# Four-layer scan network: where VectorE's side work stands beside each scan, which buffer takes the product with C, and how finely the side work is cut

## The chip, the cores and the metric

The kernel runs on one core of a Trainium2 chip. The metric is device time in microseconds (us) of one launch. PE is TensorE, DVE is VectorE, ACT is ScalarE, POOL is GpSimd, SP is SyncE, which issues all the DMAs here. Each engine executes its own instructions strictly in the order in which the program lists them; an instruction that waits holds up everything behind it on its engine.

## The reference

Four images of 64 x 64 pixels with 96 channels go through four layers. Each layer is a token mixer and a feed-forward, both with a residual:

```
x = x + conv_ref(ln_c(x))          # layer 0: gated linear recurrence; layers 1-3: selective scan
t = t + ffn_ref(ln_t(t))           # quantised 96 -> 384 -> 96 with relu
```

The mixer of layers 1 to 3 projects 96 channels to 192 plus a gate z, applies a 3x3 depthwise convolution and silu, and then runs four scans over the 4096 pixels: two pixel orders (by rows, by columns), each in both directions. Each of 192 channels has 16 states:

```
def step(h, inp):
    u_l, dl, b_l, c_l = inp
    dA = jnp.exp(dl[..., None] * A)
    h = dA * h + (dl * u_l)[..., None] * b_l[:, :, None, :]
    y = jnp.einsum('bkdn,bkn->bkd', h, c_l)
    return (h, y)
```

The four results are added, normalised, gated with silu(z) and projected back to 96 channels.

## The kernel before, in words

**Tiles of the scan.** A scan tile covers 128 rows (two halves of 64 channels, one in each pixel order), 1024 pixels and one of the 16 states. One image and layer has 2 directions x 4 segments x 3 chunks x 16 states = 384 tiles. A stage is one image in one layer; 3 layers x 4 images make 12 stages, and `scans` (lines 855 to 1036) runs all 12 x 384 = 4608 tiles in one loop over k. `CHUNKS` says which channels and pixel order the halves of the three chunks have.

**One tile on the engines.** SP broadcasts C's row of this state from DRAM into the buffer `c` (`c_rows`, two DMAs). ACT makes `da` = exp(delta x A) (`decays`). PE spreads B's row over the partitions into PSUM `bc` (`b_rows`, two matmuls). DVE multiplies `bc` by `du` in place, which I call the product, and runs the scan into `h` (both in `scan`). ACT copies the scan's last column to `carry`, for the next segment (`carry`). POOL multiplies h by c (`times_c`), here in place into h. PE adds the result into the accumulator `acc` (`accumulate`, eight matmuls), and after 16 states ACT copies `acc` out and SP stores it (`store`).

**Order in the loop.** In pass k the program emits, in this order: carry(k-1), C's rows and decays of k+2, B's rows of k+1, the product and the scan of k, times_c(k-1), sometimes a store, then the side work, then accumulate(k-2). All engines go in order, so on DVE the side work of pass k stands behind scan k and ahead of product k+1; on PE it stands between B's rows of k+1 and accumulate(k-2).

**Side work.** Three things are generators that hand out a few instructions and then `yield`: `prepare_chunk` (delta and du of the next chunk), `next_segment` (projections to B and C of the next segment), and the job. A pass takes one piece of each of the first two, and `work()` takes pieces of the job. The job of a stage, `between(im, layer)`, is everything that lies between two scans for the next image: joining the four results (`join_orders`, chain `joins`), norm, gate and output projection (`mixer_out`), `feed_forward`, then `take_in` and `convolve`. Up to three chains of it run side by side. `Job.step` adds `rate` to a credit in each pass (1.4, or 1.9 for the last feed-forwards; the credit is capped at 2.0), and every whole credit pumps each chain once. So a `yield` more in a chain means one round more, and `rate` is rounds per tile. A piece that needs a PSUM bank yields `True` and is only taken when one is free.

**The end of a job.** At item 22 of 24 of a stage, state 4 (tile 356), lines 999 to 1003 take all of the job that is left at once, with no scans between. The last image's feed-forward, which follows the last scan, has nothing beside it. The feed-forwards of images 0 and 1 in layer 3 are jobs that open once stage 10's own job is done, that of image 2 is in stage 11 behind them, that of image 3 runs after all scans (line 1282). What is left of jobs after the last tile runs in lines 1034 to 1036.

**Buffers.** `sb(n, tag, ...)` takes the next of n buffers in turn, and waits until the readers of its last use are done. h has four, freed by accumulate; c has four, freed by times_c. POOL's times_c writes over h, so it also has to wait until ACT has read h for the carry.

**Layer 0.** `gated` (lines 1039 to 1262) runs 32 strips x 12 tiles in a similar loop. From tile 96 on it has the job of image 0 beside it, at the default rate of 1.4.

## Time and profile before

| | us |
|---|---|
| median of 3 runs | 20146.27 (20117.64 to 20146.91) |
| the profiled execution's own time | 20152.58 |
| its span, first to last instruction | 20150.8 |
| DVE busy in it | 17808.5 (88%) |
| POOL busy in it | 15531.3 (77%) |
| PE busy in it (matmul records) | 16417.6 (81%) |
| ACT busy in it | 12295.0 (61%) |
| first wide scan starts, last one ends | 1890.3, 19679.4 |

The span has three parts: layer 0 with the first preparation up to 1890 us; the 4608 scan tiles, 17,789 us; and 471 us after the last scan, in which DVE is nearly idle. Rows of groups read: line, engine, operation, output <- inputs with shapes, count | busy us, mean ns of one | idle us of that engine just before them, and what ended it. All instructions are issued by a helper in line 80, so groups are told apart by the names of tiles.

### The profile page before, as it was taken

The page shows a single profiled execution, that of the slowest core. Times are in us where ns is not written, and L with a number is a line of the kernel's source. Part 1 is how long each engine was busy: PE and PEld are TensorE (multiplying, and loading weights), DVE is VectorE, ACT ScalarE, POOL GpSimd, SP SyncE. Part 2 cuts the span into 40 slices and gives each one's busy share as a digit, 9 for nine tenths or more (in the row PEclk, how much of TensorE's full clock was granted, in tenths as well). Part 3 has the DMA queues.
Part 4 walks back from the last instruction along what each step waited for, and adds up shares of the span by engine and source line. Part 5 has one row for each costly group of instructions (what it writes and reads, how often), then busy time and mean ns, then how long its engine had stood idle before and what let it go on. Part 6 is the DMA issues. An engine that isn't in the chain of part 4 may idle for free. (4 is left out here: it accounts for less than half of the span.)

```text
span 20150.8 us, 220842 instructions
## 1 busy us (share of the span) xinstructions
PE 16417.6 (81%) x70656; PEld 4838.3 (24%) x70656; DVE 17808.5 (88%) x13848; ACT 12295.0 (61%) x19373; POOL 15531.3 (77%) x10470
## 2 busy tenths in 40 slices
PE   8998788787888787788788888788788888887776
PEld 3332121121122222222222222222222222222223
DVE  6665999999999998999999999989999999999881
ACT  4444665665665665665665666666666666666553
POOL 3434888888888887888888888878888888878882
PEclk9898796786887797897887887887887887888775
DMA  0002666666666666666666676666676666676661
GB/s 20 16 18 69 165 181 174 166 186 167 168 184 171 164 179 175 166 182 180 167 187 171 167 189 167 169 180 169 170 187 171 168 187 168 170 188 161 172 169 44
DMA packets 1234532, 3148.68 MB, mean 156 GB/s; under 512 B 428049, under 2 KB 428177, under 8 KB 1227217
## 3 DMA queue, kind: packets, MB, share of 16 engines
q1 hardware_dynamic: 1233360, 3134.55, 58.6%
q8 instruction: 554, 9.08, 0.2%
q14 instruction: 618, 5.05, 0.1%
HBM read 2819.18 MB, written 314.57 MB: 156 GB/s over the span
## 5 line engine op out<-in xcount | busy, mean ns | idle before, releaser
L80 POOL TENSOR_TENSOR h<-h,c 128x1024 f32<-128x1024 f32 x4608 | 10834.6, 2358 | 2827.5 <-ACT carry L80 1727.5
L80 DVE TENSOR_TENSOR_SCAN h<-da,carry,bc 128x1024 f32<-128x1024 f32 x4608 | 10814.5, 2347 | 608.7 <-POOL carry L80 10.3
L80 PE MATMUL acc<-h,stacked 64*64 64x512 f32 x36864 | 6179.1, 747 | 498.7 <-POOL h L80 493.8
L80 ACT ACTIVATE da<-delta,decay 128x1024 f32<-128x1024 f32 x4608 | 5280.9, 1147 | 1648.9 <-DVE h L80 1601.8
L80 DVE TENSOR_TENSOR bc<-du,bc 128x1024 f32<-128x1024 f32 x4608 | 5574.5, 1210 | 611.2 <-PE bc L80 586.0
L80 PE MATMUL bc<-bs,sel 96*128 96x512 bf16 x9216 | 3346.9, 451 | 2071.8 <-DVE h L80 2054.6
L80 ACT COPY carry<-h 128x1 f32<-128x1 f32 x3456 | 649.0, 188 | 3533.7 <-DVE h L80 3529.1
L80 PEld LDWEIGHTS <-sel 96*128 96x128 bf16 x9216 | 551.3, 101 | 6988.6 <-DVE h L80 5085.7
L80 PEld LDWEIGHTS acc<-h,stacked 64*64 64x64 f32 x36864 | 1132.5, 153 | 3286.5 <-issue 1699.7
L80 ACT ACT_TABLE_LOAD x1133 | 1453.6, 1283 | 41.6 <-DVE mv L80 22.5
L80 POOL TENSOR_TENSOR c<-h,c 128x512 f32<-128x512 f32 x384 | 485.7, 1265 | 970.5 <-ACT c L80 614.8
L80 PE MATMUL conv<-pad,tap_lo 128*128 128x512 f32 x1728 | 917.5, 630 | 0.0
L80 PE MATMUL dt_proj<-rows,w 12*128 12x512 f32 x1152 | 828.0, 805 | 0.0
L80 ACT ACTIVATE du<-e,ones 128x1024 f32<-128x1024 f32 x576 | 660.8, 1147 | 228.8 <-POOL delta L80 223.2
L80 PE MATMUL x_proj_b<-u,xp 128*108 128x512 f32 x1152 | 671.9, 699 | 94.3 <-DMA xp<-in_ssm 59.0
L80 ACT ACTIVATE c<-c,l_bias 128x512 f32<-128x512 f32 x384 | 263.5, 686 | 753.0 <-PE c L80 737.9
L80 POOL TENSOR_TENSOR delta<-delta,du 128x1024 f32<-128x1024 f32 x288 | 679.5, 2359 | 12.1 <-ACT du L80 12.1
L80 POOL TENSOR_TENSOR e<-e,du 128x1024 f32<-128x1024 f32 x288 | 679.4, 2359 | 2.4 <-ACT du L80 2.4
L80 POOL TENSOR_TENSOR du<-delta,u 128x1024 f32<-128x1024 f32 x288 | 679.4, 2359 | 0.7
L80 POOL TENSOR_TENSOR delta<-delta,e 128x1024 f32<-128x1024 f32 x288 | 678.5, 2356 | 0.1
L80 PE MATMUL x_proj_c<-u,xp 128*48 128x512 f32 x1152 | 624.3, 655 | 64.3 <-ACT rows L80 64.3
L80 PE MATMUL conv<-pad,tap_hi 128*128 128x512 f32 (+1 forms) x1152 | 638.5, 650 | 8.2 <-ACT u L80 8.2
(155 smaller groups left out, 16118.3 us busy)
## 6 DMA issues: line engine op xcount, KB each, us to landing
c<-cs SPq DMA_DIRECT2D x9216, 256.0 KB, 4.1
u<-u SPq DMA_DIRECT2D x288, 512.0 KB, 7.6
y<-y SPq DMA_DIRECT2D x1152, 128.0 KB, 2.4
y<-y SPq DMA_DIRECT2D x144, 512.0 KB, 5.6
xr<-x SPq DMA_DIRECT2D x224, 192.0 KB, 4.8
u<-u SPq DMA_DIRECT2D x288, 128.0 KB, 4.4
pad<-y SPq DMA_DIRECT2D x288, 128.0 KB, 4.6
z<-zl SPq DMA_DIRECT2D x96, 256.0 KB, 2.0
```

The lines of the kernel that those rows point to most:

```text
L80: ins = f(*a, **k).ins
```

## The change

The edits, in groups:

- DVE's order: the side work of pass k is emitted between the product and the scan of k (`beside()`), no longer behind the scan. The log calls of the norms stand behind carry and decays; the start values of a chunk's carry are set at state 8 of the chunk before (`start`).
- Buffers: times_c writes into c, not h. So h is freed by times_c and the carry, and has three buffers; c is freed by accumulate, and has six. accumulate lags the scan by three tiles, not two; the loop is one pass longer.
- Finer side work: the norm's statistics are handed out two groups at a time, with the aggregates in a piece of their own; empty yields are added in `join_orders`, `mixer_out`, `feed_forward`, `first`. The rates go from 1.4 to 1.65, from 1.9 to 2.6, and in layer 0 from 1.4 to 2.6; the cap of the credit from 2.0 to 3.0.
- Smaller things: the four POOL additions of the bias in `feed_forward` become one with a broadcast operand; its result x2 shares the single buffer `xh`; the second chunk's halves are swapped, so that C needs 32 projected rows, not 48, and B's selection matrix 128 columns, not 192; `stacked` is a part of `twice`. In layer 0 h has three buffers and c six.

The diff, cut to its core (the addresses of the swapped halves and the host's packing of the weights are left out):

```diff
-CHUNKS = (((0, 0), (64, 1)), ((0, 1), (64, 0)), ((128, 0), (128, 1)))
+CHUNKS = (((0, 0), (64, 1)), ((64, 0), (0, 1)), ((128, 0), (128, 1)))
...
 NB3 = 96
-NC3 = 48
-XPW = NB3 + 2 * R + NC3
+NC2 = 2 * NS
+XPW = NB3 + 2 * R + NC2
...
-        n: ctx.enter_context(tc.tile_pool(name=f"sb{n}", bufs=n)) for n in (1, 2, 3, 4, 5, 13)
+        n: ctx.enter_context(tc.tile_pool(name=f"sb{n}", bufs=n)) for n in (1, 2, 3, 4, 5, 6, 13)
...
-    sel = const("sel", [NB3, NS, 192], BF16)
+    sel = const("sel", [NB3, NS, 128], BF16)
     for n in range(NS):
-        for k in range(3):
-            at = NS * (k % 2) + n
+        for k in range(2):
+            at = NS * k + n
             dve.tensor_copy(
                 sel[:, n, 64 * k : 64 * k + 64], mod32[:, at : at + 1].to_broadcast([NB3, 64])
...
-    def moments(src, width):
-
-        st = sb(5, "st", [128, G, 6])
-        mv = sb(5, "mv", [128, G, 2])
-        for g in range(G):
-            dve.bn_stats(st[:, g, :], src[:, g, 0:width])
-        for g in range(G):
-            dve.bn_aggr(mv[:, g, :], st[:, g, :])
-        return mv
...
@@ -226,7 +214,14 @@
 
         def measure(self, src, width, e):
 
-            mv = moments(src, width)
+            st = sb(5, "st", [128, G, 6])
+            mv = sb(5, "mv", [128, G, 2])
+            for g in range(G):
+                dve.bn_stats(st[:, g, :], src[:, g, 0:width])
+                if g % 2:
+                    yield
+            for g in range(G):
+                dve.bn_aggr(mv[:, g, :], st[:, g, :])
             yield
             act.activation(self.v, mv[:, :, 1], AF.Identity, bias=small[e])
...
             release()
             yield pair == 0
+        yield
...
         yield
         normalise(yt, yt, DI, norm.r, norm.nm)
+        yield
         yield True
...
                 pool.tensor_tensor(v[0:m], v[0:m], z[0:m], ALU.mult)
-                yield m == 64
+                yield
+        yield True
         ps = bank("out_proj")
         for q in range(G):
...
             pe.matmul(o, g[1][0:64, t], w[0:64, W_OUT + C : W_OUT + 2 * C], start=False, stop=True)
             yield
+        yield
         x1 = sb(2, "x1", [128, G, C])
         dve.tensor_tensor(x1, xr, ps[:, 0 : G * C].rearrange("p (g c) -> p g c", g=G), ALU.add)
         release()
...
         sp.dma_start(out=yc, in_=im.y[2, 0:64, t])
         sp.dma_start(out=yr[0:64], in_=im.y[0, 0:64, t])
-        sp.dma_start(out=yr[64:128], in_=im.y[1, 64:128, t])
+        sp.dma_start(out=yr[64:128], in_=im.y[1, 0:64, t])
...
         yield
         xh = sb(1, "xh", [128, G, C])
         normalise(xh, x1, C, norm.r, norm.nm)
+        yield
         yield True
         ps = bank("ff_xt")
         transpose_strip(ps, xh, 0, C)
+        yield
+        yield
         yield
         xq = sb(1, "xq", [C, MM], F8)
         dve.tensor_copy(xq, ps[0:C], saturate=False)
...
         pool.tensor_copy(hq[:, 2, :], late, saturate=False)
+        yield
         yield True
         ps = bank("ff_y")
...
         yield
-        for g in range(G):
-            pool.tensor_tensor(y[:, g, :], y[:, g, :], b[:, 3 : 3 + C], ALU.add)
-        yield
-        x2 = sb(1, "x2", [128, G, C])
+        pool.tensor_tensor(y, y, b[:, None, 3 : 3 + C].to_broadcast([128, G, C]), ALU.add)
+        yield
+        x2 = sb(1, "xh", [128, G, C])
         pool.tensor_tensor(x2, x1, y, ALU.add)
+        yield
         yield
         sp.dma_start(out=tokens(dst, s), in_=x2)
         if layer < 3:
+            yield
             norm = hold["norm", s] = Norm()
             yield from norm.measure(x2, C, 1e-6)
...
                     )
                 load_y(im, 0, hold)
+            yield
             yield
...
         def step(self):
-            self.credit = min(self.credit + self.rate, 2.0)
+            self.credit = min(self.credit + self.rate, 3.0)
...
@@ -752,7 +757,7 @@
             sp.dma_start(out=sg.us[c], in_=item.im.u[c, :, t])
         weights[item.layer].load_xp()
         sg.bs = sb(2, "bs", [NB3, T], BF16)
-        sg.cs = dram.tile([NC3, T], F32, tag="cs", name="cs")
+        sg.cs = dram.tile([NC2, T], F32, tag="cs", name="cs")
...
+        def start(i):
+            if i.first:
+                carries[i.chunk] = sb(2, f"carry{i.chunk}", [128, NS])
+                pool.memset(carries[i.chunk], 0.0)
+            i.carry = carries[i.chunk]
...
-            c = live[k, "c"] = sb(4, "c", [128, T])
+            c = live[k, "c"] = sb(6, "c", [128, T])
             for half in range(2):
-                row = NS * (CHUNKS[i.chunk][0][1] + half) + n
+                row = NS * half + n
...
-        def scan(k):
+        def scan(k, beside):
             i, n = tiles[k]
             da, b = live.pop((k, "da")), live.pop((k, "b"))
-            if n == 0 and i.first:
-                carries[i.chunk] = sb(2, f"carry{i.chunk}", [128, NS])
-                pool.memset(carries[i.chunk], 0.0)
-            i.carry = carries[i.chunk]
             dve.tensor_tensor(b, i.du, b, ALU.mult)
-            h = live[k, "h"] = sb(4, "h", [128, T])
+            beside()
+            h = live[k, "h"] = sb(3, "h", [128, T])
...
-            h, c = live[k, "h"], live.pop((k, "c"))
-            pool.tensor_tensor(h, h, c, ALU.mult)
+            c = live[k, "c"]
+            pool.tensor_tensor(c, live.pop((k, "h")), c, ALU.mult)
...
-            h = live.pop((k, "h"))
+            h = live.pop((k, "c"))
...
-        for k in range(last + 4):
+        for k in range(last + 5):
...
-                if n == 11:
-                    logarithms()
+                if n == 8 and nxt is not None:
+                    start(nxt)
                 if n == 8 and nxt is not None and nxt.d == 1:
                     nxt.yf = sb(2, "y", [128, T])
                     sp.dma_start(out=nxt.yf, in_=nxt.im.y[nxt.chunk, :, nxt.seg * T : (nxt.seg + 1) * T])
-            if 0 <= k - 1 <= last:
-                carry(k - 1)
-            if k + 2 <= last:
-                c_rows(k + 2)
-                decays(k + 2)
-            if k + 1 <= last:
-                b_rows(k + 1)
-            if k <= last:
-                scan(k)
-            if 0 <= k - 1 <= last:
-                times_c(k - 1)
-            if k >= 3 and (k - 3) % NS == NS - 1:
-                store(items[(k - 3) // NS])
-            if k <= last:
+            def beside():
                 pump(chain)
                 pump(segment)
                 if n == 13:
@@ -1028,8 +1023,24 @@
                     if item.chunk == 2:
                         drain(segment, work)
                 work()
-            if 0 <= k - 2 <= last:
-                accumulate(k - 2)
+
+            if 0 <= k - 1 <= last:
+                carry(k - 1)
+            if k + 2 <= last:
+                c_rows(k + 2)
+                decays(k + 2)
+            if n == 11:
+                logarithms()
+            if k + 1 <= last:
+                b_rows(k + 1)
+            if 0 <= k - 1 <= last:
+                times_c(k - 1)
+            if k >= 4 and (k - 4) % NS == NS - 1:
+                store(items[(k - 4) // NS])
+            if k <= last:
+                scan(k, beside)
+            if 0 <= k - 3 <= last:
+                accumulate(k - 3)
...
-            y = sb(4, "h", [C, MM])
+            y = sb(6, "c", [C, MM])
...
-            h = t["h"] = sb(4, "h", [128, T])[:, 0:MM]
+            h = t["h"] = sb(3, "h", [128, T])[:, 0:MM]
...
-            c = sb(4, "c", [128, T])[:, 0:MM]
+            c = sb(6, "c", [128, T])[:, 0:MM]
...
-        gated(images, Job(between(images[0], 0), patience=1), pl0)
+        gated(images, Job(between(images[0], 0), 2.6, patience=1), pl0)
...
-            jobs[-1].append(Job(between(im, layer - 1), 1.4))
+            jobs[-1].append(Job(between(im, layer - 1), 1.65))
 
         for im in {10: images[:2], 11: images[2:3]}.get(at, ()):
-            jobs[-1].append(Job(between(im, 3, im.dst), 1.9))
+            jobs[-1].append(Job(between(im, 3, im.dst), 2.6))
```

## Prediction

> **What bounds the kernel now.** I read the page first: shares of the engines, then the costliest groups and their idle time.
>
> ```profile
> PE 16417.6 (81%) x70656; PEld 4838.3 (24%) x70656; DVE 17808.5 (88%) x13848; ACT 12295.0 (61%) x19373; POOL 15531.3 (77%) x10470
> ...
> L80 POOL TENSOR_TENSOR h<-h,c 128x1024 f32<-128x1024 f32 x4608 | 10834.6, 2358 | 2827.5 <-ACT carry L80 1727.5
> L80 DVE TENSOR_TENSOR_SCAN h<-da,carry,bc 128x1024 f32<-128x1024 f32 x4608 | 10814.5, 2347 | 608.7 <-POOL carry L80 10.3
> ...
> L80 DVE TENSOR_TENSOR bc<-du,bc 128x1024 f32<-128x1024 f32 x4608 | 5574.5, 1210 | 611.2 <-PE bc L80 586.0
> ```
>
> DVE is the bound while scans run. Its idle time there has two sources of like size: 608.7 us before scans, of which almost none has a releaser (608.7 / 4608 = 0.13 us each), and 611 us before products, nearly all for B's rows from PE. The chain of waits (DVE, 1890 to 19679 us) shows how little else there is:
>
> ```profile
> DVE bc L80 <- PE bc L80: 586.0, 352, 18.0
> DVE xq L80 <- PE ff_xt L80: 24.0, 27, 1.8
> DVE bc L80 <- POOL du L80: 23.3, 1, 23.3
> ```
>
> All DVE waits over 0.15 us sum to 678 us, by stage 46, 30, 28, 74, 48, 49, 47, 77, 48, 51, 71, 109. The same tile of each stage has the same wait. Two of them on the timeline, first DVE and PE in tile 62 of stage 5:
>
> ```profile
> 9435.18 1.21 DVE L80 TENSOR_TENSOR bc<-du,bc 128x1024 f32<-128x1024 f32 x1
> 9436.52 2.35 DVE L80 TENSOR_TENSOR_SCAN h<-da,carry,bc 128x1024 f32<-128x1024 f32 x1
> 9444.34 1.23 DVE L80 TENSOR_TENSOR bc<-du,bc 128x1024 f32<-128x1024 f32 x1 [5.47 <-PE bc L80]
> ```
>
> ```profile
> 9433.31 0.60 PE L80 MATMUL bc<-bs,sel 96*128 96x512 bf16 x2
> 9438.41 0.74 PE L80 MATMUL out_proj<-w,u 128*128 128x96 f32 x2 [4.50 <-POOL u L80]
> ...
> 9443.59 0.71 PE L80 MATMUL bc<-bs,sel 96*128 96x512 bf16 x2
> ```
>
> PE stands still in the job (the output projection waits 4.50 us for POOL's gate product), and the next B rows stand behind it. Then PE and POOL in tile 300:
>
> ```profile
> 10350.95 1.00 PE L80 MATMUL bc<-bs,sel 96*128 96x512 bf16 x2
> 10355.93 1.99 PE L80 MATMUL acc<-h,stacked 64*64 64x512 f32 x8 [3.98 <-POOL h L80]
> ```
>
> ```profile
> 10348.93 2.36 POOL L80 TENSOR_TENSOR e<-e,du 128x1024 f32<-128x1024 f32 x1
> 10351.23 1.07 POOL L80 COPY cols_a<-u 128x512 f32<-128x512 f32 x1
> 10352.14 1.29 POOL L80 COPY part_c<-u 64x256 f32<-64x256 f32 x2
> 10353.52 4.66 POOL L80 TENSOR_TENSOR h<-h,c 128x1024 f32<-128x1024 f32 x2
> ```
>
> POOL lags by a row of side work, accumulate(k-2) waits 3.98 us, B's rows again stand behind (2.2 us on DVE). Undisturbed tiles start 3.60 us apart (median); 4608 x 3.60 = 16,589 of the 17,789 us, the other 1,200 are 678 of waits and 522 of side work on DVE. After the last scan there is a stretch with next to no DVE work:
>
> ```profile
> 19680.00:20151.00 471.00, 278.73 (x1348) 170.13 (x1340) 47.64 (x225) 174.68 (x380) 120.97 (x282) 0.51 0.16 39
> ```
>
> **The change part by part**
>
> *The tail.* By the rounds, image 2's last feed-forward has 336 before, some 118 of them run by the last tile (62 tiles x 1.9), and 218 follow alone. In the timeline of SP its last store is at 19858.8 us, and image 3's loads start at 19859.3 and end in the last store at 20147.7. So 179 us of the tail is a job left over. With rate 2.6 the three jobs (337, 347, 359 rounds) end in tiles 89, 228 and 372 of stage 11, before the last scan. Image 3 then waits for the last tile: POOL 2.4, accumulate 1.1 to 2, the copy of acc about 1.0, the store 2.4 us to landing, together 8; x2 in the buffer of xh makes the next strip wait for its store (2.2 us to landing), at most 8 x 2 = 16, of which I take 12, less 8 x 0.5 for the one POOL addition: 8 + 12 - 4 = 16 in all, and 16 - 179 = -163.
>
> *Job work moved into the scans.* The 218 rounds' DVE work, about 20 us (47.6 us for both jobs of the tail), +20.
>
> *Side work between product and scan.* The 0.13 us before a scan is the wait for its own product: 9435.18 + 1.21 = 9436.39, and the scan starts at 9436.52. Following the emission, 578 tiles had DVE side work before; 884 have it after, since statistics are cut finer. In these the piece fills the gap. After a non-scan the next independent instruction follows within about 0.03 us (norm aggregates to product: median 0), so 0.10 us each: -88. The Trainium skill (VectorE: DVE Perf Modes, Terms, DRAIN) speaks against it: every DVE instruction is followed by a flush, and the next can't issue until the pipe is empty. Then a piece in between would fill nothing, and the sum were 0. But a product follows an independent scan with no gap at all (9425.71 + 2.35 is 9428.06, and the next starts at 9427.97): only the dependent pair pays. I take the row, and keep 0 for the range.
>
> *What that place costs.* There the piece must have its inputs 2.48 us (0.13 + 2.35) earlier in its tile, and the scan is queued behind it, then ACT's carry and decays, then POOL. I took from the timeline each such piece's producer and compared its end with the end of the product: late in 76 of 106 xq (159 us in sum), 43 of 84 statistics of yt (47), 32 of 83 sums with out_proj (36), 12 of 190 `rows` (20). That is 262 us if nothing else moved. But the yields put two more rounds ahead of xq (1.2 tiles, 4.4 us, at 1.65) and one ahead of the next two (0.6 tile, 2.2 us); only `rows` has none. I count 20 to 40 of it.
>
> *PE's stalls.* The yields stand exactly where PE waited: ahead of the projection (5.5 us a stage in tile 62), of ff_y (3.7), of ff_xt (tiles 56, 118, 154: 6.2; the xq waits of 40, 55, 153: 3). accumulate(k-3) has a further 3.6 us, over the 4.0 of tile 300 but for a rest (2.2 us and some smaller ones, 2 to 4). The carry's start value leaves the queue of scan 224 (1.6). So of 48 us about 23 go; 25 stay: PE's bursts of joins and 16 accumulates at a chunk's start, convolutions, the loads at a job's start. The 12 leftover rounds taken at once in stages 3 and 7 (18.0 us each) end, as the jobs now finish in tile 346. Stages 0 to 10: 568 to about 260, the new waits included. Stage 11 keeps 95 of 109, since it gets the work of 866 old rounds, not 648. Together -323. From the same place two bounds: no stall ends, 0, and nearly all do, -580.
>
> *Three buffers of h.* Scan k now waits for times_c(k-3). In the trace of before times_c ended later than that scan's start in 20 of 4608 tiles, by 18.6 us together; POOL loses the 1727.5 us wait for the carry, so I take 0, up to +19. *Six of c:* C's rows of k+2 wait on SP for accumulate(k-4), no longer for times_c(k-2) (8547 us of SP's waits); SP's job loads are queued behind. They have 3 tiles, 11 us, to land in 4.1: 0. Where PE is late they come late too, but then DVE waits for B first.
>
> *POOL.* The product's form is the same (writing c costs as h: in layer 0 c<-h,c 512 wide is 1265 ns). Four additions of 367 ns become one like x<-x,ff_y, 910 ns: 0.56 us x 128 = 72 us, hidden under DVE, but for the tail counted above. The Trainium skill (SBUF — State Buffer, SBUF: two separate sides) has an exclusive lock between GpSimd and a DVE instruction with two SBUF inputs. The scan took 2345 to 2356 ns whatever POOL did, with one input in PSUM, so an earlier product costs 0.
>
> *Smaller C, swapped halves, selection:* 16 fewer output rows in 512-column matmuls, a 128 KB store in place of 192 KB; 0, beside scans.
>
> *Layer 0.* Its last scan ends at 1739 us, and the job's convolutions run on to 1835 before the first preparation (to 1890). At 2.6 the 479 rounds end near tile 280. But PE is busy 323 of 340 us there without the job, so the 78 us of PE work that came after the loop mostly lengthens it: I take -40, from 0 to -100. Six c buffers may help, POOL lags there too; within that range.
>
> Sum: -163 + 20 - 88 - 323 - 40 = -594, from 20152.6 us of the profiled execution to 19559. That execution lies 6 us above the median of the runs shown, so 19550.
>
> **The rivals**
>
> *PE stalls change place only.* Rates rise as the yields do: 1.65 x 469/558 is 1.39 old rounds a tile against 1.4, so PE's bursts stay, and its clock (0.82 granted) may sink as tiles close up. Then 678 stays: -163 + 20 - 88 - 40 = -271, about 19875. For it: half of the 48 us a stage are bursts; against it: the longest waits are those that the yields split.
>
> *Nearly all stalls go*, and layer 0 takes the job for nothing: -580 - 100 - 88 - 163 + 20 = -911, about 19240. Against it: PE at 81%.
>
> *Slower: DVE itself waits for side work with the scan behind.* 884 pieces stand at the head of a scan. They cancel everything at 594 / 884 = 0.67 us each; at 0.9 us the time is 20150 + 200, about 20350. It would need the 262 us above to triple although yields were added; with two or three rounds a tile a producer may fall in the same tile. Stage 11 at 2.6 is the place.
>
> *The change doesn't do what it says:* the emission shows pieces between product and scan in 884 tiles, so only its effect is open.
>
> **How the numbers follow.** Forecast 0.64, no stall ended 0.18, nearly all 0.12, slower 0.05, cancelled to within 0.2% (about what a measurement can tell from no change) 0.01. The forecast's own range is 19380 to 19720; the range reaches to most of the second case and the edge of the third: 19340 to 19820. Faster 0.94, same 0.01, slower 0.05.
>
> **What would show it.** Right: the last scan ends about 310 us before the end; idle before scans falls to about 520 us; DVE's wait for B's rows falls from 586 to about 300; POOL no longer waits for carry; the first wide scan starts near 1850. Wrong: xq, st, x or rows waits of over 100 us; scans that wait for POOL's c; the wait for B's rows still near 586.

## The result, and the profile after

The changed kernel takes 19,823.5 us (median of 4 runs, 19,815.2 to 19,851.6), the kernel before it 20,135.9 us beside it: a ratio of 0.9848, 95% interval [0.9832, 0.9864]. That is 312 us less, where 596 were forecast; the time lies 3.5 us above the range. The profiled execution of the changed kernel is the longest of its four, 28 us over their median, so spans below are compared with spans. "The scan part" is the stretch from the first wide scan's start to the last one's end in that profiled execution.

The page after, the row of engines and the three groups that answer to those of before (columns as there):

```profile
PE 16411.2 (83%) x70656; PEld 4815.3 (24%) x70656; DVE 17714.5 (89%) x13832; ACT 12300.6 (62%) x19398; POOL 15487.4 (78%) x10086
...
L78 POOL TENSOR_TENSOR c<-h,c 128x1024 f32<-128x1024 f32 (+1 forms) x4992 | 11327.0, 2275 | 3532.4 <-DVE h L78 1479.8
L78 DVE TENSOR_TENSOR_SCAN h<-da,carry,bc 128x1024 f32<-128x1024 f32 x4608 | 10797.2, 2343 | 532.1 <-POOL c L78 17.0
...
L78 DVE TENSOR_TENSOR bc<-du,bc 128x1024 f32<-128x1024 f32 x4608 | 5567.8, 1208 | 499.7 <-PE bc L78 473.6
```

POOL's first releaser is now the scan and no longer ACT's carry. (The group holds layer 0's narrow products too, hence the mean of 2275 ns.) Idle time before scans fell from 608.7 to 532.1 us, about as forecast. DVE's wait for B's rows fell from 586.0 to 473.6 us only; about 300 was forecast.

DVE's chain of waits between the first wide scan and the last (1963 to 19,560 us; total, times, longest, in us):

```profile
DVE bc L78 <- PE bc L78: 473.6, 295, 22.2
DVE rows L78 <- ACT bs L78: 29.6, 15, 3.9
DVE x L78 <- PE out_proj L78: 29.3, 24, 2.9
DVE st L78 <- ACT yt L78: 22.0, 22, 2.7
DVE h L78 <- POOL c L78: 17.0, 16, 2.0
```

Behind B's rows there is a row of small waits for side work (rows, x, st); the kernel before had 41 us of DVE's waits for side work in its scan part, this one has 117. The windows after the last scan (us; busy of PE, PEld, DVE, ACT, POOL; PE's granted clock, DMA share, GB/s):

```profile
19560.00:19850.00 290.00, 174.32 (x864) 107.90 (x864) 30.23 (x144) 104.00 (x227) 66.68 (x137) 0.51 0.19 46
```

The tail has 290 us, where it had 471. The 301 us between the two spans are the sum of three parts, in us:

| | before | after | difference | forecast |
|---|---|---|---|---|
| up to the first wide scan | 1890 | 1963 | +72 | -40 |
| 4608 scan tiles | 17,789 | 17,597 | -192 | -391 |
| after the last scan | 471 | 290 | -181 | -163 |

Inside the scan part DVE's busy time (overlapped time counted once) fell by 81 us, its gaps under 0.15 us by 98, and its longer waits by 14 only (654 to 640; the prediction's 678 counts the 23.3 us ahead of the first wide scan too). The last is where the forecast had -323.

### The profile page after: what moved, and what is told of

The parts are those of the page before. It is cut to its first block, busy times and chain, and to the rows that moved or that the text cites. A ratio compares the mean times of both kernels' runs of the same rounds, so it can differ in the third digit from the quotient of the medians.

```text
span 19849.8 us, 224201 instructions
## 1 busy us (share of the span) xinstructions
PE 16411.2 (83%) x70656; PEld 4815.3 (24%) x70656; DVE 17714.5 (89%) x13832; ACT 12300.6 (62%) x19398; POOL 15487.4 (78%) x10086
## 5 line engine op out<-in xcount | busy, mean ns | idle before, releaser
L78 POOL TENSOR_TENSOR c<-h,c 128x1024 f32<-128x1024 f32 (+1 forms) x4992 | 11327.0, 2275 | 3532.4 <-DVE h L78 1479.8
L78 DVE TENSOR_TENSOR_SCAN h<-da,carry,bc 128x1024 f32<-128x1024 f32 x4608 | 10797.2, 2343 | 532.1 <-POOL c L78 17.0
L78 PE MATMUL acc<-c,twice 64*64 64x512 f32 x36864 | 6212.0, 750 | 21.8 <-POOL c L78 21.7
L78 DVE TENSOR_TENSOR bc<-du,bc 128x1024 f32<-128x1024 f32 x4608 | 5567.8, 1208 | 499.7 <-PE bc L78 473.6
L78 PE MATMUL bc<-bs,sel 96*128 96x512 bf16 x9216 | 3392.6, 456 | 2350.8 <-DVE h L78 2239.7
L78 PEld LDWEIGHTS acc<-c,twice 64*64 64x64 f32 x36864 | 1132.6, 153 | 2805.1 <-issue 1888.6
L78 PE MATMUL x_proj_c<-u,xp 128*32 128x512 f32 x1152 | 632.0, 662 | 76.0 <-ACT rows L78 67.1
L78 PE MATMUL conv<-pad,tap_hi 128*128 128x512 f32 (+1 forms) x1152 | 597.5, 620 | 0.6 <-ACT u L78 0.4
L78 DVE TENSOR_TENSOR_SCAN h<-da,l_carry,bc 128x512 f32<-128x512 f32 x384 | 491.5, 1280 | 42.1 <-POOL c L78 2.0
```

The lines of the kernel that those rows point to most:

```text
L78: ins = f(*a, **k).ins
```

## The experiments

Each time below is the median of 4 runs (12 of `bufs_old`, 7 of `behind_bufs_old`). Of the kernel before, 20,133 to 20,141 us were measured beside them. Each ratio is to those runs. Scan parts and waits come from one profiled execution of each kernel. Five kernels whose code for the scan part is the changed kernel's (itself and the four of the section on layer 0) have scan parts of 17,560 to 17,597 us and waits of 604 to 640, so differences of some 40 us between two kernels say little.

### What places the waits: buffers, place and yields

**The old buffers in the changed kernel** (`bufs_old`), and the same with the old place of the side work (`behind_bufs_old`):

```diff
-            c = live[k, "c"]
-            pool.tensor_tensor(c, live.pop((k, "h")), c, ALU.mult)
+            h, c = live[k, "h"], live.pop((k, "c"))
+            pool.tensor_tensor(h, h, c, ALU.mult)
...
-            if 0 <= k - 3 <= last:
-                accumulate(k - 3)
+            if 0 <= k - 2 <= last:
+                accumulate(k - 2)
```

(with four h and four c buffers). Expected:

> The changed kernel with the buffers of before in the scans (product with C in place into h, four of h, four of C, accumulate two tiles behind); the side work stays between product and scan, yields and rates stay as changed. Theory 'buffers pay': GpSimd again waits for the carry, TensorE's accumulate again waits for GpSimd (2.6 us a stage before), and scans wait for a free h; the scan part grows from 17,597 to 17,650 to 17,720 us, total 19880 to 19950. Rival 'buffers are idle': nothing on VectorE's path was ended by them, total 19824 within 30.

> As the run before, and the side work behind the scan again: of the change only yields, rates and the small things are left. If place and buffers add up, the total is that of the last run plus 138 us (what the place alone brought: 19961 against 19824). Against the kernel before, 20141, what is left then is the tail (-180) and layer 0 (+72) and what the yields bring in the scans: if they end the 23 us a stage that the forecast named, 17,789 falls to about 17,550 and the total is 19790; if new stalls take their place, the scan part stays within 40 of 17,789 and the total is about 20030.

Measured: 20,135.4 us, ratio 1.0002 [0.9994, 1.0011], so the whole gain is gone; and 20,189.9, ratio 1.0029 [1.0017, 1.0040]. Without the buffers that I had put down at 0 the change brings nothing, although its tail is as short (293 us in both). The groups of the page of `bufs_old`:

```profile
L78 POOL TENSOR_TENSOR h<-h,c 128x1024 f32<-128x1024 f32 x4608 | 10836.0, 2359 | 2849.9 <-ACT carry L78 1873.1
...
L78 DVE TENSOR_TENSOR bc<-du,bc 128x1024 f32<-128x1024 f32 x4608 | 5570.5, 1209 | 802.8 <-PE bc L78 770.9
```

POOL waits for the carry again, and DVE's wait for B's rows is 771 us, not 474. The run with old buffers and old place keeps of the change the yields, the rates and the small things: its scan part is 17,900 us against 17,789 before, and its waits are 750, not 654. So these cost 111 us, if anything more: the profiled execution is the fastest of its seven. With the old buffers the new place is worth next to nothing in the scan part (17,884 against 17,900), and 54 us by the medians, where 138 had been expected.

**The new buffers in the kernel before** (`before_bufs`): the reverse edit, with the small things of the change, the old place, yields, rates and cap.

> The kernel before with the changed buffers alone (product with C into c, three of h, six of C, accumulate three tiles behind) and the small things that make room for them; yields, rates and the side work behind the scan as before. Scan part before 17,789 us. Theory 'buffers pay by themselves': as between the two kernels with side work behind the scan (17,900 to 17,701), 150 to 250 us less, scan part near 17,590, total about 19,940 against 20,135; layer 0 (1890) and tail (471) stay. Rival 'buffers only repair what the new rates broke': scan part within 40 of 17,789, total 20,100 or more.

Measured: 19,859.8 us, ratio 0.9864 [0.9850, 0.9879], 274 us less, most of the 312 that the whole change brings. In its scan part (17,528 us) the waits are 395 us, not 654, though every piece of side work falls in the same tile as before. Two groups of its page, and the first of them in the page of before:

```profile
L78 PE MATMUL acc<-c,twice 64*64 64x512 f32 x36864 | 6114.8, 739 | 8.5 <-POOL c L78 8.5
L78 DVE TENSOR_TENSOR bc<-du,bc 128x1024 f32<-128x1024 f32 x4608 | 5569.6, 1209 | 358.0 <-PE bc L78 332.7
```

```profile
L80 PE MATMUL acc<-h,stacked 64*64 64x512 f32 x36864 | 6179.1, 747 | 498.7 <-POOL h L80 493.8
```

PE's wait for POOL's product ahead of accumulate is gone (493.8 to 8.5 us), and DVE's wait for B's rows falls from 586.0 to 332.7. From the end of a scan to the start of its product on POOL it took 1.24 us in the median before, and over 3.6 us, a whole tile, in 16% of the tiles; here it takes 0.14 us, and over 3.6 us in 5%. Tile 62 of stage 5, which the prediction shows, is one case. DVE, then PE, then POOL on the timeline:

```profile
9321.87 1.21 DVE L78 TENSOR_TENSOR bc<-du,bc 128x1024 f32<-128x1024 f32 x1
...
9327.60 1.23 DVE L78 TENSOR_TENSOR bc<-du,bc 128x1024 f32<-128x1024 f32 x1 [2.04 <-PE bc L78]
```

```profile
9321.41 0.74 PE L78 MATMUL out_proj<-w,u 128*128 128x96 f32 x2 [1.63 <-POOL u L78]
```

```profile
9314.88 2.38 POOL L78 TENSOR_TENSOR c<-h,c 128x1024 f32<-128x1024 f32 x1 [1.15 <-DVE h L78]
...
9320.10 1.26 POOL L78 TENSOR_TENSOR u<-u,zl 128x512 f32<-128x512 f32 x1
```

The same tile of before, POOL:

```profile
9429.59 4.69 POOL L80 TENSOR_TENSOR h<-h,c 128x1024 f32<-128x1024 f32 x2
...
9437.08 1.28 POOL L80 TENSOR_TENSOR u<-u,zl 128x512 f32<-128x512 f32 x1
```

Before, POOL runs two products back to back, late by one, and its gate product `u` starts 1.9 us after the tile's product on DVE (9435.18). With the buffers POOL has caught up (it even waits 1.15 us for a scan), and `u` starts 1.8 us ahead of the tile's product. PE's wait in the output projection falls from 4.50 to 1.63 us and DVE's from 5.47 to 2.04, with no yield added.

**The buffers, but accumulate two tiles late** (`lag_two`), in the changed kernel:

```diff
-            if 0 <= k - 3 <= last:
-                accumulate(k - 3)
+            if 0 <= k - 2 <= last:
+                accumulate(k - 2)
```

> The changed kernel, but accumulate two tiles behind the scan as before, not three; the product still goes into c. Tells the two halves of the buffer change apart. If it is the later accumulate (TensorE no longer stands before a product that GpSimd still owes), the 290 us of the old buffers come back here: scan part 17,800 to 17,880, total 20,030 to 20,110. If it is the product's own buffer (GpSimd no longer waits for the carry), the scan part stays near 17,600, total 19,824 within 40.

Measured: 19,879.5 us, ratio 0.9873 [0.9858, 0.9888]: 56 us more than the changed kernel, and 256 us under the one with the old buffers. PE's wait for POOL ahead of accumulate is 128 us in it (22 in the changed kernel). Most of the buffers' worth is thus what `lag_two` keeps: the product's buffer of its own, with the numbers of buffers. These two were not run apart, so what the two c buffers more are worth alone is open. The later accumulate is the rest, and a small one: the two intervals still touch.

**The old place in the changed kernel** (`behind`): `beside()` is called after the scan.

```diff
-            beside()
             h = live[k, "h"] = sb(3, "h", [128, T])
...
                 op1=ALU.add,
             )
+            beside()
```

> The changed kernel, but the side work stands behind the scan again, all else as changed. Expected by 'place pays': the gap of 0.13 us before 884 scans comes back (98 us) and the overlap of a product's start with its scan's end is lost there again (some 60 us), while the new waits of VectorE for its own side work (statistics of yt, out_proj, rows, xq: about 9 us a stage, 60 in stage 11, together 150) go: total within 60 us of 19824. If those waits are the loss against the forecast: about 100 faster, 19720. If stalls of TensorE come back in their place: 100 slower, 19920.

Measured: 19,961.3 us, ratio 0.9914 [0.9899, 0.9929]; 138 us more by the medians and 104 in the scan part of the profiled executions. Against the changed kernel its short gaps (under 0.15 us) are 112 us more (600, not 488) and DVE's busy time 81 more; its waits are 90 less (550, not 640), since those for side work go from 117 to 7. What the place gains besides the gap is seen in the changed kernel's DVE timeline:

```profile
9341.19 1.23 DVE L78 TENSOR_TENSOR bc<-du,bc 128x1024 f32<-128x1024 f32 x1
9342.33 0.68 DVE L78 CAST xq<-ff_xt 96x512 fp8e5<-96x512 f32 x1
9342.93 2.33 DVE L78 TENSOR_TENSOR_SCAN h<-da,carry,bc 128x1024 f32<-128x1024 f32 x1
9345.18 1.20 DVE L78 TENSOR_TENSOR bc<-du,bc 128x1024 f32<-128x1024 f32 x1
```

The piece starts 0.09 us before the product's recorded end, the scan 0.08 before the piece's, and the next product 0.10 before the scan's. This tile takes 3.99 us, an undisturbed one 3.60: the 0.68 us piece costs 0.39. The same kind of piece in `behind`:

```profile
9372.49 1.23 DVE L78 TENSOR_TENSOR bc<-du,bc 128x1024 f32<-128x1024 f32 x1 [3.07 <-PE bc L78]
9373.85 2.35 DVE L78 TENSOR_TENSOR_SCAN h<-da,carry,bc 128x1024 f32<-128x1024 f32 x1
9376.12 0.66 DVE L78 CAST xq<-ff_xt 96x512 fp8e5<-96x512 f32 x1
9376.70 1.22 DVE L78 TENSOR_TENSOR bc<-du,bc 128x1024 f32<-128x1024 f32 x1
```

From product to product it is 4.21 us, 0.22 more: with the piece behind the scan there are two such overlaps in the chain, not three, and the gap of 0.13 us besides.

**The new place on the old yields** (`place_old_yields`): `before_bufs` with `beside()` between product and scan, as in the changed kernel.

> The kernel before with the new buffers (product into c, three of h, six of c, accumulate three tiles late), now also with the side work between product and scan; the old yields, rates and cap are kept, so every piece of side work falls in the same tile as before. Theory A (the place is worth the filled gap less the lost overlap, and the old rounds leave the pieces' inputs early enough): as where the place was moved alone under the new yields, small gaps -112, DVE busy +82, waits in the scan part from 395 by some 20: -90 to -140, so about 19,740 from the 19,860 of the same kernel with the place behind. Theory B (the new yields are what makes this place possible; without them statistics, xq and sums wait for their producers with the scan queued behind, up to the 262 us counted from the trace of before): waits for side work rise from 37 to 200 or more, 19,850 to 20,000. The wait for side work before products tells the two apart.

Measured: 19,901.9 us, ratio 0.9885 [0.9870, 0.9900]; by the medians 42 us above `before_bufs`. The chain of waits, DVE:

```profile
DVE bc L78 <- PE bc L78: 297.0, 193, 19.1
DVE xq L78 <- PE ff_xt L78: 85.0, 56, 3.9
DVE st L78 <- ACT yt L78: 71.5, 33, 5.1
DVE st L78 <- POOL xh L78: 30.6, 31, 2.3
DVE x L78 <- PE out_proj L78: 29.3, 17, 5.0
```

Waits for side work are 243 us (37 in `before_bufs`), close to the 262 that the prediction counted in the trace of before for the case that nothing else moved. One of them, on DVE and then on PE:

```profile
9555.76 1.21 DVE L78 TENSOR_TENSOR bc<-du,bc 128x1024 f32<-128x1024 f32 x1
9560.61 0.69 DVE L78 CAST xq<-ff_xt 96x512 fp8e5<-96x512 f32 x1 [3.65 <-PE ff_xt L78]
9561.22 2.33 DVE L78 TENSOR_TENSOR_SCAN h<-da,carry,bc 128x1024 f32<-128x1024 f32 x1
```

```profile
9559.06 1.52 PE L78 MATMUL ff_xt<-ident,xh 128*96 128x128 f32 x4 [4.50 <-ACT xh L78]
```

The scan stands 3.65 us behind a cast whose transpose PE has only just made. Theory B held: at this place the pieces come too early for their inputs on the old yields. With the new ones the waits for `xq` are 12 us in the changed kernel, not 85.

**The tail on top, at the exact old rhythm**, with the new place (`place_old_yields_tail`) and with the old one (`bufs_tail`); the diff is against `place_old_yields`:

```diff
-            self.credit = min(self.credit + self.rate, 2.0)
+            self.credit = min(self.credit + self.rate, 3.0)
...
-            jobs[-1].append(Job(between(im, layer - 1), 1.4))
+            jobs[-1].append(Job(between(im, layer - 1), 4 / 3 + 1e-9))
...
-            jobs[-1].append(Job(between(im, 3, im.dst), 1.9))
+            jobs[-1].append(Job(between(im, 3, im.dst), 2.5))
```

> The same kernel with the last feed-forwards alone at 2.5 rounds a tile (cap 3.0); the jobs of the steady stages keep the exact rhythm of before (1, 1, 2 rounds), which the run with the tail alone had changed. By the rounds the three end in tiles 76, 187 and 291 of stage 11. Theory A (the new yields and rates bring nothing; buffers, place and tail are the whole gain): a tail of about 292 and so -179 from the run beside it, +20 to +60 of denser side work in stage 11; about 19,600, some 220 below the changed kernel. Theory C (the new yields and rates are worth something where place and buffers are already there): no lower than the changed kernel's 19,824. If the run beside it follows B, the time is that run's less 120 to 160.

> The kernel before with the new buffers, the side work behind the scan, the old yields and the old rhythm in the steady stages, and the last feed-forwards at 2.5 rounds a tile. With the place between product and scan the same shortening of the tail (469 to 289 us) brought nothing, since stage 11's waits rose from 102 to 236 us. Theory B (those waits are pieces that stand at the head of a scan before their inputs are there): behind the scan they do not arise, stage 11 keeps its 58 us of waits but for 40 to 80 of PE's bursts, and the time is 19,720 to 19,780. Theory D (a stage cannot hold the last jobs' work at 2.5 old rounds a tile, wherever the pieces stand): waits of stage 11 rise by 130 as there, about 19,850.

Measured: 19,909.7 us, ratio 0.9890 [0.9874, 0.9907], and 19,830.8, ratio 0.9853 [0.9836, 0.9869]. The first is no faster than the same kernel with the long tail: the tail fell by 180 us (469 to 289), and stage 11's waits rose from 102 to 236 us, stage 10's from 61 to 86. With the side work behind the scan stage 11's waits rose from 58 to 157. So about 100 us goes with the denser work in either place, and a further 35 with the new place alone; the expectation's two theories had 40 to 80 and 130 for the old place. DVE's waits in stage 11 (about 18,080 to 19,620 us) with the new place:

```profile
DVE xq L78 <- PE ff_xt L78: 93.0, 20, 8.7
DVE x L78 <- PE out_proj L78: 56.4, 19, 6.4
DVE bc L78 <- PE bc L78: 53.7, 21, 12.3
```

and with the old one (18,000 to 19,500 us):

```profile
DVE bc L78 <- PE bc L78: 84.0, 35, 13.1
DVE xq L78 <- PE ff_xt L78: 41.9, 19, 6.5
DVE x L78 <- PE out_proj L78: 23.4, 10, 5.1
```

These runs fill a square. The scan part in us, all with the new buffers and the short tail:

| | old yields and rates | new yields and rates |
|---|---|---|
| side work behind the scan | 17,647 (`bufs_tail`) | 17,701 (`behind`) |
| between product and scan | 17,739 (`place_old_yields_tail`) | 17,597 (changed kernel) |

Either edit alone is a loss (+92 and +54); both together gain 50 us. The profiled execution of `bufs_tail` lies 20 us under its median and that of the changed kernel 28 over it; if these distances lie in the scan part, the three figures are about +72, +36 and -98, with the same signs. In each row the yields come with another rhythm of the rounds, so their figures hold an effect of alignment that no run here takes apart (see the next section); in each column the rhythm is the same, and the place is the only difference. And `bufs_tail`, without either edit, can't be told from the changed kernel in its time (0.9853 against 0.9848, intervals [0.9836, 0.9869] and [0.9832, 0.9864]): what the changed kernel gains in the scan part it loses in layer 0, where its wide scans start 90 us later (1963, not 1873 us).

### The pace of the side work

The cap of 2.0 had cut the rate of 1.4 to 4/3 rounds a tile (1, 1, 2, 1, 1, 2 ...) and that of 1.9 to 1.5. The cap of 3.0 leaves 1.65 whole and cuts 2.6 to 2.5. Since `take_in` and `convolve`, the job's second half, got no yields but one, their work became denser: 1.65 rounds a tile, not 1.33. `second_slow` returns the second half to 1.52:

```diff
+            self.late, self.phase = late, 0
...
+                    self.phase += 1
+                    if self.phase == 3 and self.late:
+                        self.rate = self.late
...
-            jobs[-1].append(Job(between(im, layer - 1), 1.65))
+            jobs[-1].append(Job(between(im, layer - 1), 1.65, late=1.52))
```

> The changed kernel, but the job's second half (take_in, convolve, which got no yields) runs at 1.52 rounds a tile instead of 1.65; before it was 1.33, since the cap of 2.0 cut 1.4 to 4/3. Theory 'denser second half': the stalls of in_xt for its normalised rows (3.5 us a stage), of accumulate for ACT's copy of acc (2.9) and part of TensorE's bursts ease: 4 to 8 us a stage less, total 19740 to 19780. Rival 'position': the stalls only move with the emission, total 19824 within 30.

Measured: 19,804.6 us, ratio 0.9835 [0.9821, 0.9850], 19 us under the changed kernel by the medians, which the two intervals don't separate and which the expectation gave to the rival "position". The waits of the scan part are 573 us; kernels with the changed kernel's own pace have 604 to 640.

**The short tail in the kernel before, by rates alone** (`before_tail`: cap 3.0, steady jobs at 4/3, the last at 2.2), and **the old rates from another start of the credit** (`before_phase`):

```diff
-            self.rounds, self.rate, self.credit = rounds, rate, 0.0
+            self.rounds, self.rate, self.credit = rounds, rate, 0.7
```

> The kernel before with nothing changed but the rates: the cap of the credit 3.0, the usual rate 4/3 (what 1.4 came to under the cap of 2.0), and the last feed-forwards at 2.2 (1.5 under the cap), so that image 2's ends in tile 356 of the last stage. The tail should fall from 471 to about 290 us, and the scan part grow by 20 to 60 (more side work in the last stage): total 19980 to 20020 against 20141. Rival: the work costs in the scans what it cost after them, total 20100 or more.

> The kernel before, with the job's credit starting at 0.7 instead of 0: the same rates and rounds, 2-1-1 per three tiles instead of 1-1-2, so every piece of side work falls on other tiles. Theory 'alignment': the stalls of the kernel before (48 us a stage) depend on which pieces fall together; with rates that differed by this rhythm alone they were 76 a stage (before_tail). Then the scan part moves by 100 to 350 us, total 20,230 to 20,480 or, if it is as good, within 100 below. Rival 'each stall is its piece's own': total within 40 of 20,135.

Measured: 20,329.8 us, ratio 1.0098 [1.0082, 1.0113], and 20,429.3, ratio 1.0146 [1.0131, 1.0161]: slower by 195 and 296 us. In `before_tail` the tail fell to 292 us, and still the kernel lost. The plain 4/3, rounded just below the whole number, makes the rhythm drift (1, 1, 1, 2, 1, 1, 2 ...), at the same density. DVE's waits in its scan part:

```profile
DVE bc L80 <- PE bc L80: 779.0, 348, 30.7
DVE xq L80 <- PE ff_xt L80: 88.8, 30, 5.5
DVE x L80 <- PE out_proj L80: 37.0, 19, 5.1
```

Stages 4, 5, 6, 8 and 9 have 76.5 us of waits each, against 48.4 before. In `place_old_yields_tail`, where the rhythm was kept exactly, they have 38.7 against 39.2 of the same kernel without the tail. So which pieces of three generators meet in one tile decides as much as how many there are. Of three alignments of the old work with the old buffers, the kernel before has the best; how far the kernels with the new buffers move with theirs was not run.

### Layer 0

Four runs look for the cause of its +72 us. First, the statistics of its norm in one piece (`l0_stats_whole`):

```diff
-                if g % 2:
+                if g % 2 and split:
                     yield
...
-            yield from norm.measure(st.xr, C, 1e-6)
+            yield from norm.measure(st.xr, C, 1e-6, False)
```

> The changed kernel, but in layer 0's preparation the four statistics and their aggregates are again one piece (two rounds fewer per strip). In the changed kernel a layer-0 tile takes 4.55 us even before the job begins (tiles 0 to 96), against 4.2 before the change. Theory 'position': the two added rounds push the preparation's projections to a place where TensorE stalls. Then tiles 24 to 96 go back to about 4.2 us, the first wide scan starts near 1840 to 1860 instead of 1962 us, and the total is about 110 us under the changed kernel's 19824, 19715. Rival 'buffers' (three h buffers, the strip's result in the buffer of c): tiles stay at 4.55 us, total 19824.

Measured: 19,737.5 us, ratio 0.9801 [0.9784, 0.9817], 86 us under the changed kernel. A tile between 24 and 96, ahead of the job, takes 4.14 us (before 4.21, changed 4.55), and the first wide scan starts at 1863 us. DVE's chain of waits from 100 to 440 us, changed kernel and then this one:

```profile
DVE da L78 <- PE bc L78: 60.3, 24, 5.7
```

```profile
DVE da L78 <- PE bc L78: 38.7, 14, 4.5
```

Then the same with two empty yields ahead of the whole statistics (`l0_empty_yields`):

```diff
+            if not split:
+                yield
+                yield
             for g in range(G):
                 dve.bn_stats(st[:, g, :], src[:, g, 0:width])
-                if g % 2:
+                if g % 2 and split:
                     yield
```

> The changed kernel; in layer 0's preparation the norm's statistics stand in one piece, as before, but two empty yields stand ahead of them, so that the preparation has as many pieces as in the changed kernel. With the statistics whole and no empty yields the time was 86 us lower (tiles 24 to 96 at 4.14 us, not 4.55). If it is the number of pieces (everything behind them falls in later tiles): as the changed kernel, 4.5 us a tile, about 19,824. If it is the cutting of DVE's work itself (a scan behind each half): as with whole statistics, 4.15 us a tile, about 19,740.

Measured: 19,848.8 us, ratio 0.9857 [0.9842, 0.9872]; 4.55 us a tile again. It is the number of pieces in the preparation, not the cutting of DVE's work: all that stands behind comes two pieces later. Which later meeting costs the time, the runs don't show.

The rate of the job in layer 0 (`l0_rate`, 1.65 for 2.6) and more h buffers there (`l0_h_halves`, two half-width tiles in one buffer) were tried as causes:

```diff
-        gated(images, Job(between(images[0], 0), 2.6, patience=1), pl0)
+        gated(images, Job(between(images[0], 0), 1.65, patience=1), pl0)
```

```diff
+        spare = []
...
-            h = t["h"] = sb(3, "h", [128, T])[:, 0:MM]
+            if spare:
+                h = t["h"] = spare.pop()[:, MM:T]
+            else:
+                spare.append(sb(3, "h", [128, T]))
+                h = t["h"] = spare[0][:, 0:MM]
```

> The changed kernel, but the job beside layer 0 runs at 1.65 rounds a tile, not 2.6 (2.5 with the cap). In the changed kernel tiles 96 to 300 take 5.15 us on average, and the last 84 4.4 to 4.6. If only the work itself counts (TensorE is busy over 90%), the job's 120 us are spread over more tiles and the first wide scan stays at 1962 us within 15, total 19824. If bursts of two and three rounds a tile cost (theory 'dense'), the loop gets shorter by 40 to 60 us: first wide scan at 1905 to 1925, total 19770. If a job that is left over at the loop's end costs more than it did beside it, it starts later than 1962.

> The changed kernel, but layer 0 takes h as halves of the three wide buffers, so that six tiles of h are live instead of three. Rival 'buffers': tiles 24 to 96 fall from 4.55 to about 4.2 us and the total to about 19715. Theory 'position': no change, 4.55 us and 19824.

Measured: 19,823.5 us, ratio 0.9844 [0.9829, 0.9859], and 19,831.8, ratio 0.9847 [0.9832, 0.9862]; the first wide scan starts at 1963 and 1960 us. With the lower rate layer 0's loop ends at 1782 us, not 1912, and the job's rest then takes the time that was saved. Neither is the cause.

### The best of both

`best1` is the changed kernel with layer 0's statistics whole and the second half of the jobs at 1.52.

> The changed kernel with layer 0's statistics in one piece (19,737 alone, -86) and the second half of the job at 1.52 rounds a tile (19,805 alone, -20). If they add up: 19,717.

Measured: 19,689.6 us, ratio 0.9777 [0.9760, 0.9793], 134 us under the changed kernel, somewhat more than the sum of the two edits (86 and 19). This version beats both kernels.

## Why the prediction was half right

That half of the forecast gain came is in part luck: the stalls of PE, put at -323, did not shrink, and the buffers, put at 0, brought what stands in the scan part instead. Term by term:

- **The tail: right.** The stretch is 181 us shorter (163 forecast), and its work lengthens DVE's busy time with side work by 25 us (20 forecast). What the forecast gave too small a price is the density of that work in stage 11: the forecast kept 95 us of waits there, and the changed kernel has 131.
- **The gap between product and scan: the mechanism held, the term was mis-sized.** "0.10 us each: -88" became 112 us of filled gaps and 81 less of DVE's busy time, 193 / 884 = 0.22 us each. The forecast let 0.03 of the gap's 0.13 us stand; the rows show the gap filled whole, and one overlap of 0.09 us more in the chain. A term of 0, by the Trainium skill's rule (VectorE: DVE Perf Modes, Terms, DRAIN), is not what these rows show: the cast and the scan behind it start 0.09 and 0.08 us before the recorded end of what stands ahead. That row was read alone: the same page, under The DRAIN you can't avoid, adds that a next instruction that is not held starts earlier.
- **What that place costs: too small.** "I count 20 to 40 of it" was 117 us of waits for side work in the scan part, where `behind` has 7. The count of 262 us for the case that nothing moves was sound (243 in `place_old_yields`), and with the new yields and rates half of it goes.
- **PE's stalls, -323: the step that failed.** The stalls that it names did end in the changed kernel. Per stage of 4, 5, 6, 8 and 9 the projection to `xq` went from 6.1 to 0 us, the gate product's from 4.65 to 1.8, `hq` from 3.7 to 0, accumulate's wait for POOL from 2.6 to 0: together 15 us, and with the waits for `xq` (2.7) and for the carry's start (1.6), which ended too, 20 of the 23 forecast. (A late B row can stand behind several waits of PE, so how a stage's sum is shared among them is an estimate; the sum is not.) New ones of the same size came: the input's transpose 3.5, ACT's copy of y 2.9, st 2.7, rows 2.7, x 2.3, the norms 1.8, POOL's c 1.8. The stage stayed at 50.2 us (48.4 before). With the yields and rates on the old buffers and at the old place (`behind_bufs_old`) the stalls of `xq`, `hq` and the gate product are nearly gone too, and yet the stage has 59.0 us: the step was wrong by itself, and it is the buffers that hid it in the changed kernel. The rival "PE stalls change place only" described this, and its 19,875 was nearer to the result, though it too had the buffers at 0. One of the new ones on PE, and DVE behind it, in the changed kernel:

```profile
10318.22 1.52 PE L78 MATMUL in_xt<-ident,xh 128*96 128x128 f32 x4 [2.21 <-ACT xh L78]
...
10321.59 1.03 PE L78 MATMUL bc<-bs,sel 96*128 96x512 bf16 x2
```

```profile
10322.66 1.23 DVE L78 TENSOR_TENSOR bc<-du,bc 128x1024 f32<-128x1024 f32 x1 [3.40 <-PE bc L78]
```

  The step asked where each old stall would go, and not what the moved pieces would meet. `before_tail` and `before_phase` show that a stage's sum moves by more than half with the rhythm alone. PE's granted clock is a rival that no run takes apart from this: over the span it was 0.817 before, 0.814 in the changed kernel, 0.821 in `before_bufs` and 0.809 in `bufs_old`, and a matmul for B's rows took 451, 456, 451 and 457 ns. So it did not simply sink as tiles closed up (`before_bufs` has the highest of these); what its differences of 1.5% are worth is open.
- **Buffers, 0: wrong.** They are worth 199 us in the scan part with the old place (17,900 against 17,701) and 287 with the new one (17,884 against 17,597), with the small things on both sides. The step asked only who would wait for the new buffers (17 us, as forecast). It read the 1727.5 us of POOL's waits for the carry as idle time of an engine that is not the bound; but behind POOL's product stand POOL's pieces of the job, behind these PE, and behind PE the B rows.
- **Layer 0, -40: wrong in sign, by one edit.** Without the two pieces more the start of the scans came 27 us earlier than before, near the forecast; with them 72 later. The step weighed the job's rate and not the preparation's own pieces.
- **Cap of the credit:** the rival's "1.65 x 469/558 is 1.39 old rounds a tile against 1.4" left out that the cap had cut 1.4 to 1.33, and that the second half got none of the yields. The "62 tiles x 1.9" left out the cap too: at 1.5 they are 93 rounds, not 118.

The sum of the scan part by the runs: 17,789 + 111 (yields, rates and small things, with the tail's work) - 199 (buffers) - 104 (place) = 17,597 us. It is one order of the edits, and the sizes hang on it: the buffers and small things first bring 261 us of the scan part (`before_bufs`), and place ahead of buffers 15. The smaller C, the swapped halves and the single addition were not run by themselves; inside `before_bufs` they are part of its 274 us.

## What to carry to other kernels

An engine that is not the bound can still be late: ask of each of its waits what is queued behind it and whom that feeds, before it is called free; a buffer of its own for a product (here about 250 us, with two c buffers more) can do what finer cutting of the work doesn't. Where side work is dealt out by a rhythm, test an edit against the same rhythm, since the alignment alone moved the kernel before by 1.5%. Two edits that each lose (a place ahead of the scan; more yields) can gain together, so run the square and not only the sum.

## What was not expected of the hardware

- DVE's neighbours that don't depend on each other overlap by 0.08 to 0.10 us in the records, and the dependent pair product and scan has a gap of 0.13 us. An independent piece put between them saved 0.22 us, not 0.13.
- The scan took 2343 to 2347 ns on average in all these kernels, whether POOL's product wrote in place or into another buffer, and whether it ran early or late.
